# Hybrid Mamba, mixture-of-experts and gated-attention block: the softplus of later groups summed by accumulating transfers, the experts' weight rows issued from ACT, and new priorities for the planner

## The chip, the cores and the metric

One core of one Trainium2 chip. The metric is the device time of one execution in microseconds. Engines are named as in the profile: PE is TensorE, DVE is VectorE, ACT is ScalarE, POOL is GpSimd, SP is SyncE, which only issues transfers. Each engine runs its own list of instructions strictly in order; a transfer that is issued by an engine stands in that engine's list, and the engine waits there until what the transfer needs is ready.

## The reference, cut to what matters

The input is x with 8 sequences of 256 tokens and 128 features, all in float32. Four blocks follow each other, each added to its own input after a layer norm:

1. a selective state-space block (Mamba): RMS norm, a projection to 2 x 256 channels, a causal convolution of 4 taps, a SiLU, a projection to a time step and to B and C (16 states), and a recurrence over the 256 tokens;
2. a mixture of 8 experts with inner width 352, the best 2 per token;
3. a gated attention unit with squared-ReLU scores;
4. the same mixture of experts again, with the same weights.

The part that the change touches in the first block is the softplus of the time step:

```python
delta = jax.nn.softplus(ts @ dt_w + dt_b)
def step(state, inp):
    dA = jnp.exp(A[None, :, :] * d_t[:, :, None])
    new = dA * state + d_t[:, :, None] * B_t[:, None, :] * h_t[:, :, None]
    y = jnp.einsum('bin,bn->bi', new, C_t) + D * h_t
```

and in the mixture of experts the share `w_e` of expert e in each token:

```python
inter = up_o * jax.nn.silu(gate_o)
out = out + w_e[:, None] * (inter @ w_down[e])
```

## The kernel before, in words

**Groups and lanes.** The 8 sequences form 4 groups of 2 (512 tokens). For each group the work is cut into lanes, written as Python generators that yield one operation at a time: `prelude` (s: norm, projection, convolution, time step, softplus), `recurrence` (m), `gating` (g), `ending` (f), `tail` (t: projection back) and `rest` (r: first mixture p, attention a, second mixture r). Two lanes serve all groups: `feeder` loads the rows of B and C and lets ACT make the decays, `adder` issues accumulating transfers from POOL.

**The order of the work** is decided while the program is built. `Board` keeps, for each engine, when it would be free, and for each tile when it would be ready and when its last reader would be done, from costs that are written into the operations. `Board.pick` takes the lane whose next operation could start first; lanes on the same engine that could start no later than `PATIENCE` after it compete by rank (`RANKS`, one number per kind of lane and group; the lowest wins). An ACT operation that needs another activation table than the one that is loaded is held to start `SWITCH` = 1.3 later, but only if it has been ready for less than `LONG`; both `PATIENCE` and `LONG` are 0 before. Where PE would idle ahead of an operation, `Board.do` puts small matmuls of the identity into that operation's own output bank (`fill` in `pe`, line 324; one per 0.23 of planned idle time); they compute nothing that is kept. So the number of these fills in the program tells how long the planner expected PE to idle, and where.

**The recurrence.** For 2 of the 16 states and one half of the channels at a time, DVE multiplies B by delta*h (L743), scans (L748) and multiplies by C (L752), 1024 columns each; there are 16 such steps in each group. All but the first of the results in each half are summed into the first by transfers with accumulation (`adder`, L715, POOL queue, 512 KB each; five tiles hold such states). ACT makes the decays, exp(A*delta), ahead of the scans (L696).

**Softplus.** softplus(z) is put together as relu(z) + ln(1 + exp(-|z|)), plus a term for what 1 + e loses when it is rounded. ACT makes |z| (L595), relu(z) (L603), e (L613), w = 1 + e (L617) and ln w (L627). DVE makes the lost part in one operation (L621), subtracts it from both halves of relu(z) (L623), adds ln w to both halves (L631), and multiplies by h (L632). In groups 1 to 3 these take both halves (1024 columns) at once where they can; group 0 goes by halves.

**The mixture of experts.** Expert widths are laid end to end and cut into 22 tiles of 128. For each tile `gate` (a matmul, L486, and a SiLU on ACT, L958), `up` (L984, or L991 where a tile holds the border of two experts; its product with the SiLU is made on DVE, L998) and `down` (L1004) are issued, the gate 4 tiles ahead. The input of `up` is x already scaled by the expert's share: the shares are transposed, copied by ACT (L1019) and written to a small table in device memory (`wrow`, L1022), and row e of that table is loaded into all partitions (`fetched`, L967, 256 KB) and multiplied by x on DVE (L975). Both transfers are issued by POOL. Three tiles hold such rows, so the row of expert e+3 can be loaded only after the last `up` that reads expert e, the border matmul L991 (or L984). For the mixtures named in `SOON` the row of expert 0 is made by PE instead (L931, L938).

The activation sets are two: SiLU and tanh in one, exp and ln in the other; each change is an ACT_TABLE_LOAD (L57).

Of the kernel before, what the change touches and what calls it, by code (L numbers as in the profile page):

```python
# [31 lines left out]
class Board:  # L32
# [1 line left out]


    SWITCH = 1.3
    PATIENCE, LONG = 0, 0
    FILL = 0.23

    def given(self, op):  # L40
# [32 lines left out]
    def pick(self, lanes):  # L73

        at = []
        for l in lanes:
            t = self.start(l.op)

            if self.switches(l.op) and t - self.given(l.op) < self.LONG:
                t += self.SWITCH  # L80
            at.append((t, l))
        first, lane = min(at, key=lambda x: x[0])
        near = [
            l for t, l in at if l.op.engine == lane.op.engine and t <= first + self.PATIENCE
        ]
        return min(near, key=lambda l: l.rank)


class Lane:
    def __init__(self, rank, work, after):  # L90
        self.rank, self.work, self.after, self.op = rank, work, after, None


@with_exitstack
def kernel(
# [27 lines left out]
    nc = tc.nc  # L123
# [23 lines left out]
    BEHIND = 2  # L147

    RANKS = {
# [3 lines left out]
    }  # L153
    SOON = ("p0", "p1", "r0", "p3", "r3")
    SPLIT = ()
# [116 lines left out]
        nc.gpsimd.memset(t[:, :, 0 : K - 1], 0.0)  # L272
    one = const.tile([P, 1], FP, name="one")
    nc.vector.memset(one, 1.0)


    board = Board(nc.scalar.preload_act_table_set)
# [110 lines left out]
    def layernorm(x, name, key, rms=False, parts=None):  # L388
# [13 lines left out]
        def moments_and_guard():  # L402
# [8 lines left out]

        parts = parts or [x]
        yield dve(0.46 * NT + 0.2, [st, mv, rstd], parts, moments_and_guard)
        yield pool(1.8, [rstd], [], lambda: nc.gpsimd.tensor_tensor(
            rstd.ap, rstd.ap, half[:, 0:NT], ALU.pow
        ))
        xn = ring(norm, [P, NT, H], f"xn{key}", f"xn_{name}")
# [72 lines left out]
    def biased(x, bias):  # L490

        NT = x.ap.shape[1]
        yield pool(1.2, [x], [], lambda: nc.gpsimd.tensor_tensor(
            x.ap, x.ap, bias.unsqueeze(1).to_broadcast([P, NT, H]), ALU.add
        ))

# [20 lines left out]
    def prelude(g):  # L517
# [67 lines left out]

        dl = [ring(mam, [P, G], f"dl{c}", f"dl_{g}_{c}", bufs=2) for c in range(NI)]
        ex = ring(mam, [P, NI, G], "ex", f"ex_{g}")
        for c in range(NI):  # L590
            ps = bank([P, G], f"dt_{g}_{c}")
            yield pe(mm(G), [ps], [ww], product(
                ps.ap, [(dt_w_sb[:, c * P : (c + 1) * P], xpj[:R, :])]
            ))
            yield act(act_us(G), [ex], [ps], lambda: nc.scalar.activation(  # L595
                ex.ap[:, c, :], ps.ap, AF.Abs, bias=col("dt_b", c)
            ))
            if g == 0:
                yield dve(dve_us(G), [dl[c]], [ps], lambda: nc.vector.tensor_scalar(
                    dl[c].ap, ps.ap, col("dt_b", c), 0.0, ALU.add, ALU.max  # L600
                ))
            else:
                yield act(act_us(G), [dl[c]], [ps], lambda: nc.scalar.activation(  # L603
                    dl[c].ap, ps.ap, AF.Relu, bias=col("dt_b", c)
                ))
            shut(ps)

        parts = [(c, c + 1) for c in range(NI)] if g == 0 else [(0, NI)]
        exs = [Held(ex.ap[:, a:b, :], ex.ready) for a, b in parts]
        wws = [Held(ww.ap[:, a:b, :], ww.used) for a, b in parts]  # L610
        du = [ring(mam, [P, G], f"du{c}", f"du_{g}_{c}", bufs=2) for c in range(NI)]
# [16 lines left out]
        for (a, b), w in zip(parts, wws):  # L628
            for c in range(a, b):
# [2 lines left out]
                    nc.vector.tensor_mul(du[c].ap, dl[c].ap, h[c].ap)  # L632

                yield dve(2 * dve_us(G), [dl[c], du[c]], [w, h[c]], step)
        if g > 0:

            for c in range(NI):
                yield act(act_us(G), [h[c]], [], lambda: nc.scalar.mul(h[c].ap, h[c].ap, col("D", c)))
        ex.used = max(e.used for e in exs)
        ww.used = max(w.used for w in wws)  # L640
        led_up[g] = bc, h, xT, dl, du

    def gating(g):

# [156 lines left out]
    def tail(g):  # L801
        gates.pop(g)
        bc, h, _, delta, du = led_up.pop(g)
        G = SIZES[g] * T
# [24 lines left out]
    def forked(rank, works):  # L829

        kids = [Lane(rank + (i,), w, []) for i, w in enumerate(works)]
        for l in kids:
            forks[0] += 1
            l.name = f"fork{forks[0]}"
        lanes.extend(kids)
# [107 lines left out]
    def moe(g, which, key, shared, ends):  # L943
# [20 lines left out]
        def fetched(e):  # L964

            wb = ring(ffn, [P, G], f"wb{key}", f"wb_{nm}_{e}", bufs=WB)
            yield load(3.6, [wb], [wrow], lambda: nc.gpsimd.dma_start(  # L967
                wb.ap, wrow.ap[e : e + 1, :].partition_broadcast(P)
            ), "POOL", 0.6)
            wx[e] = wb  # L970

        def weighted(e):
# [36 lines left out]
        def tile_of(i):  # L1009
# [12 lines left out]
        yield load(2.2, [wrow], [weT], lambda: nc.gpsimd.dma_start(  # L1022
            wrow.ap.rearrange("e (t p) -> (e t) p", p=P), weT.ap
        ), "POOL", 0.7)


        for i in range(LEAD):
# [210 lines left out]
    for g in range(NG):  # L1238
# [5 lines left out]
        waiting[-1].name = f"g{g}"  # L1244
        waiting.append(Lane((RANKS["f"][g], g), ending(g), [f"m{g}"]))
        waiting[-1].name = f"f{g}"
        waiting.append(Lane((RANKS["t"][g], g), tail(g), [f"f{g}", f"g{g}"] + [f"t{g - 1}"] * (g > 0)))
        waiting[-1].name = f"t{g}"
        waiting.append(Lane((RANKS["r"][g], g), rest(g), [f"t{g}"] + [f"r{g - 2}"] * (g > 1)))
# [58 lines left out]
```

## Time and profile before

| | us |
|---|---|
| median of 3 runs (764.91 to 766.28) | 766.09 |
| the profiled execution | 766.44 |
| its span on the core | 764.7 |
| busy in the span: PE / DVE / ACT / POOL | 739.0 / 569.0 / 439.3 / 129.5 |
| ACT_TABLE_LOAD, 96 in all | 123 |
| transfers, mean | 116 GB/s |

The span is what the hardware profiler saw on the core; the execution's own time is 1.7 us longer. A busy PE isn't a PE that does useful work, since the fills count as busy too: 556 of its 1591 matmuls are fills. A float32 matmul of 512 columns leaves two records in the trace, and so does a fill.

### The profile page before, as it was taken

What the parts mean: (1) busy time and instruction counts of PE and PEld (TensorE: products, weight loads), DVE (VectorE), ACT (ScalarE), POOL (GpSimd) and SP (SyncE); (2) the same over time, 40 slices, a digit from 0 to 9 for tenths busy, and PEclk for the clock granted to TensorE, in tenths of its full rate; (3) what the DMA queues carried; (4) which work ended last, traced back from release to release, by engine and by line L of the source; (5) the groups of instructions that cost most, each with busy time, mean ns of one, the idle gap of its engine ahead of it and who ended that gap; (6) DMA issues with size and microseconds to landing.
All of it is one profiled execution on the core that took longest, in us unless ns stands there. A gap on an engine that the chain in (4) does not pass through costs nothing.

```text
span 764.7 us, 8437 instructions
## 1 busy us (share of the span) xinstructions
PE 739.0 (97%) x3077; PEld 402.2 (53%) x3077; DVE 569.0 (74%) x824; ACT 439.3 (57%) x576; POOL 129.5 (17%) x177
## 2 busy tenths in 40 slices
PE   4999999999989989999999999999999999999997
PEld 3877996664326654334654443343764433454343
DVE  2599999998999988899998997996636333535332
ACT  4578334698993787997776768742062321432221
POOL 2021110421212321111222221112101100200000
PEclk9999999999999999999999999999999999999999
DMA  8619795567865435476674557665000210101110
GB/s 257 207 60 219 178 219 143 141 143 175 218 147 132 87 101 134 110 180 136 145 186 111 132 129 181 164 153 109 1 28 29 69 28 14 28 14 44 27 42 14
DMA packets 34999, 88.63 MB, mean 116 GB/s; under 512 B 4339, under 2 KB 14414, under 8 KB 34958
## 3 DMA queue, kind: packets, MB, share of 16 engines
q0 software_dynamic: 14288, 46.54, 30.0%
q1 hardware_dynamic: 20624, 41.54, 16.5%
q8 instruction: 24, 0.39, 0.2%
q14 instruction: 17, 0.14, 0.1%
q10 hardware_dynamic: 46, 0.01, 0.0%
HBM read 55.71 MB, written 1.44 MB: 75 GB/s over the span
## 4 chain that ended last, share of the span: by engine, by line
PE 65%; DVE 21%; DMA 4%; issue 4%; ACT 4%; POOL 0%; DVEq 0%; ACTq 0%; POOLq 0%
PE dn_r L1004 10%; PE gp_r L486 9%; PE dn_p L1004 8%; DVE st L748 7%; PE up_r L984 7%; PE gp_p L486 6%; PE up_p L984 5%; DVE st L743 4%; DVE st L752 4%; PE up_r L991 3%; DMA wb_p<-wrow_p 3%; PE up_p L991 3%; PE av_a L1195 1%; PE xpj L324 1%; ACT L57 1%
## 5 line engine op out<-in xcount | busy, mean ns | idle before, releaser
L748 DVE TENSOR_TENSOR_SCAN st<-decay,st 128x1024 f32<-128x1024 f32 x64 | 147.3, 2302 | 2.9
L57 ACT ACT_TABLE_LOAD x95 | 121.9, 1283 | 1.7
L696 ACT ACTIVATE decay<-dl,zero,a_sb 128x510 f32<-128x510 f32 x128 | 96.8, 806 | 42.8 <-DVE st L748 42.1
L958 ACT ACTIVATE sg_r<-gp_r,zero 128x512 f32<-128x512 f32 x88 | 60.1, 687 | 104.7 <-PE gp_r L486 92.6
L998 DVE TENSOR_TENSOR it_r<-up_r,sg_r 128x512 f32<-128x512 f32 x88 | 60.4, 687 | 66.6 <-PE up_r L984 40.7
L958 ACT ACTIVATE sg_p<-gp_p,zero 128x512 f32<-128x512 f32 x88 | 59.2, 686 | 62.8 <-PE gp_p L486 45.3
L1004 PE MATMUL dn_p<-it_p,wd_sb 128*128 128x512 f32 x176 | 91.0, 604 | 3.6 <-DVE it_p L998 3.5
L715 POOL DMA_DIRECT2D st<-st x58 | 51.0, 885 | 241.9 <-DVE st L752 199.2
L1004 PE MATMUL dn_r<-it_r,wd_sb 128*128 128x512 f32 x176 | 90.4, 601 | 0.0
L486 PE MATMUL gp_r<-xT_r,wg_sb 128*128 128x512 f32 x176 | 89.4, 594 | 0.0
L998 DVE TENSOR_TENSOR it_p<-up_p,sg_p 128x512 f32<-128x512 f32 x88 | 59.9, 685 | 39.1 <-PE up_p L984 26.0
L486 PE MATMUL gp_p<-xT_p,wg_sb 128*128 128x512 f32 x176 | 88.8, 593 | 0.0
L743 DVE TENSOR_TENSOR st<-bt,du 128x1024 f32<-128x1024 f32 x64 | 78.8, 1231 | 0.0
L752 DVE TENSOR_TENSOR st<-st,ct 128x1024 f32<-128x1024 f32 x64 | 78.1, 1220 | 0.8
L984 PE MATMUL up_p<-wb_p,wu_sb 128*128 128x512 f32 x128 | 65.4, 595 | 0.5 <-DVE wb_p L975 0.5
L984 PE MATMUL up_r<-wb_r,wu_sb 128*128 128x512 f32 x128 | 65.4, 596 | 0.0
L1004 PEld LDWEIGHTS dn_p<-it_p,wd_sb 128*128 128x128 f32 x176 | 31.6, 189 | 51.0 <-issue 35.9
L486 PEld LDWEIGHTS gp_p<-xT_p,wg_sb 128*128 128x128 f32 x176 | 33.0, 190 | 40.6 <-issue 35.9
L486 PEld LDWEIGHTS gp_r<-xT_r,wg_sb 128*128 128x128 f32 x176 | 32.9, 190 | 40.7 <-issue 35.4
L1004 PEld LDWEIGHTS dn_r<-it_r,wd_sb 128*128 128x128 f32 x176 | 31.7, 190 | 41.9 <-issue 35.5
L324 PEld LDWEIGHTS y<-ident 128*128 128x128 f32 x464 | 52.1, 192 | 1.2 <-PE dt L486 0.8
L324 PE MATMUL y<-ident 128*128 128x128 f32 x464 | 52.4, 275 | 0.0
(225 smaller groups left out, 885.1 us busy)
## 6 DMA issues: line engine op xcount, KB each, us to landing
st<-st POOLq DMA_DIRECT2D x54, 512.0 KB, 6.4
bt<-bc SPq DMA_DIRECT2D x32, 512.0 KB, 5.7
ct<-bc SPq DMA_DIRECT2D x32, 512.0 KB, 4.9
wb_r<-wrow_r POOLq DMA_DIRECT2D x30, 256.0 KB, 3.9
wb_p<-wrow_p POOLq DMA_DIRECT2D x29, 256.0 KB, 4.8
st<-h POOLq DMA_DIRECT2D x6, 256.0 KB, 3.8
wg_sb<-in_L_ffn_w_gate_dram SPq DMA_DIRECT2D x2, 704.0 KB, 4.3
wu_sb<-in_L_ffn_w_up_dram SPq DMA_DIRECT2D x2, 704.0 KB
```

The costliest lines, as they stand in the source:

```text
L57: self.load_tables(op.table)
L324: nc.tensor.matmul(ps[:, 0:n], lhsT=ident[:, 0:m], rhs=ident[:, 0:n], start=True, stop=True)
L486: nc.tensor.matmul(ps, lhsT=lhsT, rhs=rhs, start=(i == 0), stop=(i == len(terms) - 1))
L696: nc.scalar.activation(shaped[:, n, :, 1:], delta[c].ap.rearrange("p (b t) -> p b t", b=GB)[:, :, 1:], AF.Exp, bias=zero, scale=a_sb[:, c, ...
L715: yield load(us, [acc], [st], lambda: nc.gpsimd.dma_start(into, of, accum_op=ALU.add), "POOL", 0.9)
L743: yield dve(1.22, [st], [bt, du[c]], lambda: nc.vector.tensor_mul(st.ap, bt.ap, du[c].ap.unsqueeze(1).to_broadcast([P, NC, G])))
L748: yield dve(2.29, [st], [das[c]], lambda: nc.vector.tensor_tensor_scan(flat, das[c].ap.rearrange("p n t -> p (n t)"), flat, 0.0, ALU.mult, ...
L752: yield dve(1.22, [st], [ct], lambda: nc.vector.tensor_mul(st.ap, st.ap, ct.ap))
L958: yield act(act_us(G), [sg], [gp], lambda: nc.scalar.activation(sg.ap, gp.ap, AF.Silu, bias=zero), SILU)
L984: nc.tensor.matmul(ps.ap, lhsT=wu_sb[:, i * P : (i + 1) * P], rhs=wa.ap[:, cols_of], start=True, stop=True,)
L998: yield dve(dve_us(width), [it], [ps, sg], lambda: nc.vector.tensor_mul(it.ap, ps.ap, sg.ap[:, cols_of]))
L1004: yield pe(mm(dn.ap.shape[1]), [dn], [it], lambda: nc.tensor.matmul(dn.ap, lhsT=wd_sb[:, i, :], rhs=it.ap[:, cols_of], start=(i == 0), sto ...
```

## The change

1. **Softplus of groups 1 to 3.** relu(z) of both halves lies in one tile (`dl`). ACT makes w = -1 - e with a new constant `minus_one`, DVE makes (w + 1) + e, which is the lost part with its sign turned, and ACT makes ln(-w). The lost part and the logarithm are then added to `dl` by two accumulating transfers of 512 KB each, issued by POOL through `adder`, one after the other; DVE only multiplies by h once both have landed. The four DVE operations L623 and L631 go in each of these groups. Group 0 stays as it was.
2. **Rows of the experts.** The write of the table and the loads of its rows are issued by ACT instead of POOL; the planner's time for issuing goes from 0.6 and 0.7 to 0.1.
3. **The planner.** `PATIENCE` is 0.21 and `LONG` is 2.6; each lane has its own patience, which is a new number per group (`"w"`) for the lanes of `ending` and for the forked lanes; all ranks are new; the planned cost of the power on POOL is 1.45 (was 1.8) and of the bias on POOL 1.6 (was 1.2). So nearly all instructions of later stages stand in another order.

```diff
-    PATIENCE, LONG = 0, 0
+    PATIENCE, LONG = 0.21, 2.6
...
-            l for t, l in at if l.op.engine == lane.op.engine and t <= first + self.PATIENCE
+            l for t, l in at if l.op.engine == lane.op.engine and t <= first + l.patience
...
-        "s": [4, 4, 1, 2.5], "m": [1.5, 3.5, 3, 3.5],
-        "g": [2, 0, 1.5, 2], "t": [1, 0, 0, 0.5],
-        "r": [2.5, 0.5, 3.5, 2.5], "f": [1, 0, 4, 0.5], "feeder": 5, "adder": 1.5,
+        "s": [3, 2, 3.5, 2.5], "m": [3.5, 4, 4, 2.5],
+        "g": [4, 2.5, 2.5, 0.5], "t": [1, 3, 0, 0.5],
+        "r": [2.5, 1, 2.5, 2], "f": [1, 0, 4, 0], "w": [0, 0, 1.5, 0], "feeder": 5, "adder": 0,
...
-        yield pool(1.8, [rstd], [], lambda: nc.gpsimd.tensor_tensor(
+        yield pool(1.45, [rstd], [], lambda: nc.gpsimd.tensor_tensor(
...
-        yield pool(1.2, [x], [], lambda: nc.gpsimd.tensor_tensor(
+        yield pool(1.6, [x], [], lambda: nc.gpsimd.tensor_tensor(
...
-        dl = [ring(mam, [P, G], f"dl{c}", f"dl_{g}_{c}", bufs=2) for c in range(NI)]
+        both = ring(mam, [P, NI, G], "dl", f"dl_{g}", bufs=2)
+        dl = [Held(both.ap[:, c, :], both.used) for c in range(NI)]
...
+        if g > 0:
+            both.ready = max(d.ready for d in dl)
+            both.used = max(d.used for d in dl)
+            yield act(act_us(NI * G), [ex], [], lambda: nc.scalar.activation(
+                ex.ap, ex.ap, AF.Exp, bias=zero, scale=-1.0
+            ), EXP)
+            yield act(act_us(NI * G), [ww], [ex], lambda: nc.scalar.activation(
+                ww.ap, ex.ap, AF.Identity, bias=minus_one, scale=-1.0
+            ))
+            yield dve(dve_us(NI * G), [ex], [ww], lambda: nc.vector.scalar_tensor_tensor(
+                ex.ap, ww.ap, 1.0, ex.ap, ALU.add, ALU.add
+            ))
+            sums.append((f"s{g}", 6.3, both, ex, both.ap, ex.ap))
+            yield act(act_us(NI * G), [ww], [], lambda: nc.scalar.activation(
+                ww.ap, ww.ap, AF.Ln, bias=zero, scale=-1.0
+            ), EXP)
+            sums.append((f"s{g}", 6.3, both, ww, both.ap, ww.ap))
+            while landed.get(f"s{g}", 0) < 2:
+                yield None
+            du = [ring(mam, [P, G], f"du{c}", f"du_{g}_{c}", bufs=2) for c in range(NI)]
+            for c in range(NI):
+                dl[c].ready = both.ready
+                yield dve(dve_us(G), [du[c]], [dl[c], h[c]], lambda: nc.vector.tensor_mul(
+                    du[c].ap, dl[c].ap, h[c].ap
+                ))
+                yield act(act_us(G), [h[c]], [], lambda: nc.scalar.mul(h[c].ap, h[c].ap, col("D", c)))
+            led_up[g] = bc, h, xT, dl, du
+            deltas[g] = both
+            return
...
-            yield load(3.6, [wb], [wrow], lambda: nc.gpsimd.dma_start(
+            yield load(3.6, [wb], [wrow], lambda: nc.scalar.dma_start(
                 wb.ap, wrow.ap[e : e + 1, :].partition_broadcast(P)
-            ), "POOL", 0.6)
+            ), "ACT", 0.1)
...
-        yield load(2.2, [wrow], [weT], lambda: nc.gpsimd.dma_start(
+        yield load(2.2, [wrow], [weT], lambda: nc.scalar.dma_start(
             wrow.ap.rearrange("e (t p) -> (e t) p", p=P), weT.ap
-        ), "POOL", 0.7)
+        ), "ACT", 0.1)
```

The line numbers of the profile are those of the kernel before; in the changed kernel these lines stand 3 to 36 further down.

More of the change, by code (lines that the diff above doesn't have):

```diff
@@ L91, in __init__ @@
         self.rank, self.work, self.after, self.op = rank, work, after, None
+        self.patience = Board.PATIENCE
 @with_exitstack
@@ L274 @@
     nc.vector.memset(one, 1.0)
+    minus_one = const.tile([P, 1], FP, name="minus_one")
+    nc.vector.memset(minus_one, -1.0)
     board = Board(nc.scalar.preload_act_table_set)
@@ L606, in prelude @@
             shut(ps)
-        parts = [(c, c + 1) for c in range(NI)] if g == 0 else [(0, NI)]
+        if g > 0:
[27 more added lines that the diff above has]
+            return
+        parts = [(c, c + 1) for c in range(NI)]
         exs = [Held(ex.ap[:, a:b, :], ex.ready) for a, b in parts]
@@ L634, in prelude @@
                 yield dve(2 * dve_us(G), [dl[c], du[c]], [w, h[c]], step)
-        if g > 0:
-            for c in range(NI):
-                yield act(act_us(G), [h[c]], [], lambda: nc.scalar.mul(h[c].ap, h[c].ap, col("D", c)))
         ex.used = max(e.used for e in exs)
@@ L641, in prelude @@
         led_up[g] = bc, h, xT, dl, du
+        deltas[g] = both
+    deltas = {}
     def gating(g):
@@ L803, in tail @@
         bc, h, _, delta, du = led_up.pop(g)
+        deltas[g].used = max(d.used for d in delta)
         G = SIZES[g] * T
@@ L832, in forked @@
         for l in kids:
+            l.patience = RANKS["w"][rank[1]]
             forks[0] += 1
@@ L1246 @@
         waiting[-1].name = f"f{g}"
+        waiting[-1].patience = RANKS["w"][g]
         waiting.append(Lane((RANKS["t"][g], g), tail(g), [f"f{g}", f"g{g}"] + [f"t{g - 1}"] * (g > 0)))
```

## The prediction

> **What bounds the kernel now.** I read the page's 40 slices first, then the chain, then PE's fills stage by stage, then the single waits.
>
> ```profile
> PE   4999999999989989999999999999999999999997
> DVE  2599999998999988899998997996636333535332
> ACT  4578334698993787997776768742062321432221
> PE 65%; DVE 21%; DMA 4%; issue 4%; ACT 4%; POOL 0%; DVEq 0%; ACTq 0%; POOLq 0%
> ```
>
> PE looks full everywhere, yet the chain starts on DVE. The next answers split it: busy time by stage, of PE's fills alone (line 324) and of all engines.
>
> ```profile
> 0.00:128.00 128.00, 85.67 (x738) 85.03 (x738) 1.00 0.69 185
> 128.00:281.00 153.00, 31.11 (x256) 30.52 (x256) 1.00 0.62 147
> 281.00:543.00 262.00, 6.59 (x50) 6.20 (x50) 0.99 0.58 137
> 543.00:765.00 222.00, 8.49 (x68) 8.30 (x68) 1.00 0.10 29
> ...
> 128.00:281.00 153.00, 144.47 (x640) 84.12 (x640) 142.74 (x208) 121.37 (x151) 37.37 (x40) 1.00 0.62 147
> 281.00:543.00 262.00, 261.18 (x862) 116.45 (x863) 230.68 (x302) 181.71 (x223) 51.09 (x67) 0.99 0.58 137
> ```
>
> The columns of a stage are its length, PE, PE's weight loads, and in the last two lines DVE, ACT and POOL; (x) counts records, two per fill. Up to 128 us PE is mostly fills: group 0's recurrence runs on DVE alone. From 128 to 281 DVE is busy 143 of 153 us, and it is the bound. From 281 on PE is full, and the fills (118 records, 59 fills) are all that is left to win there; idle time outside them is under 1 us up to the last matmul. So the end is: when DVE lets PE start at 281, plus PE's fixed work, plus the fills after it.
>
> The waits that the change aims at, on POOL, PE and DVE in the first mixture:
>
> ```profile
> 162.53 0.56 POOL L1022 DMA_DIRECT2D wrow_p<-weT_p  x1
> 168.63 0.87 POOL L715 DMA_DIRECT2D st<-st  x1 [5.54 <-DVE st L752]
> 169.30 1.34 POOL L967 DMA_DIRECT2D wb_p<-wrow_p  x2
> 167.53 7.53 PE L324 MATMUL up_p<-ident 128*128 128x128 f32 x66
> 176.84 0.69 DVE L975 TENSOR_TENSOR wb_p<-wb_p,xT_p 128x512 f32<-128x512 f32 x1 [2.41 <-DMA wb_p<-wrow_p]
> ```
>
> The rows' load stands in POOL's list behind a state sum that waits 5.54 us for DVE; PE fills for 7.5 us and DVE waits 2.41.
>
> **The change part by part.**
>
> ```profile
> L57 ACT ACT_TABLE_LOAD x95 | 121.9, 1283 | 1.7
> L623 DVE TENSOR_TENSOR dl<-dl,ex 128x512 f32<-128x512 f32 x8 | 5.3, 689 | 0.2
> L631 DVE TENSOR_TENSOR dl<-dl,ww 128x512 f32<-128x512 f32 x8 | 5.4, 680 | 0.0
> st<-st POOLq DMA_DIRECT2D x54, 512.0 KB, 6.4
> bc<-ww SPq DMA_DIRECT2D x4, 64.0 KB, 4.8
> 1.91 0.28 ACTq L206 DMA_DIRECT2D vecs<-in_L_attn_a_conv_b_dram  x1
> L681 SPq DMA_DIRECT2D bt<-bc x32: 319/320/1638, 28.5 to 491.1; - x32
> ```
>
> *Softplus.* Four DVE operations go in each of three groups. They start 0.60 to 0.70 us apart, so 2.4 us per group. Two transfers per group come in: a 0.885 us issue on POOL and 6.4 us to land each, the second after the first, 14.6 us where DVE took 2.4. In the changed order DVE's multiply by h of group 1 stands three recurrence steps after the lost part's operation (4.79 us each, from the state sums' issues, which come 4.79 apart): 14.4 us of cover. So group 1 gains its 2.4, called 2.3, as group 0 is alone on DVE. If both landed at the 9.3 us that is the longest sum here, it would lose some 6 (2 x 10.2 - 14.4). Behind the pair on POOL two state sums wait; two spare tiles cover one more step. ACT does as many operations as before.
>
> *Middle stage.* Added up row by row from the instruction order, with the trace's spacing of starts (a recurrence step 4.7, a 512-column operation 0.60), DVE has 143.7 us of work from group 0's last gate product (127.4) to the first up product of group 1's first mixture (280.25). That took 152.9, so DVE waited 9.2. In the changed kernel the same span holds 147.8: two more scans, group 3's convolution and the dropped operations less. That is +4.1, and as much less later.
>
> Of the 9.2 us of waits, 5.9 are for expert rows (2.41 here, 0.92 at 206 and 2.59 at 280). On ACT the load no longer stands behind a state sum, but the table's write could be slower: the write from SP's list took 4.8 us for 64 KB, POOL's took 2.1 for 16 KB, so +2.7 at worst, with four SiLUs (2.7 us) between the write and the load in the new order. Gain between 0 and 5.9; I take half, 3.0, since one part of each wait is the landing itself. Nothing comes of row waits after 281, where PE stays full.
>
> *ACT's new transfers.* 59 rows and 8 tables at 0.28 (ACT's small loads) to 0.32 (SP's row broadcasts, the same form): 18.8 to 21.4 us more in ACT's list. Loads of tables fall from 96 to 80 in the order: 16 x 1.283 = 20.5 us less. Even, and ACT has 32 us of slack in the middle stage and 80 in the next. A row's wait for the border matmul now holds ACT: behind it stand SiLUs of the next gates, which PE runs after that border anyway, so 0; but 6 of the 35 rows that are issued while the recurrence runs have a table load and a decay right behind. At the mean wait of a SiLU for its gate (92.6 us in 54 waits, 1.7) these are 10 us of ACT, part of it under the three decay tiles that are made ahead. Bounds 0 and 10; I take 2.
>
> The Trainium skill (ScalarE: Activation LUTs, What ACT_TABLE_LOAD costs) counts a drain with each load, 2.66 us per switch. By it the 16 loads would be 42.6 us. The trace doesn't show the drain: a load starts at 163.42 and the next SiLU at 164.72. The skill (DMA: Bandwidth & Descriptors, Issuing engines are not separate DMA queues) also speaks against the move: another issuing engine saves only issue time. By that the 3.0 above would be 0; the 5.54 us ahead of the row's load is a wait in POOL's list, which the rule doesn't count.
>
> *POOL and traffic.* POOL loses 38.7 us of issues and gains 5.3; it is busy 17%, so nothing. The six transfers add 3.1 of 88.6 MB; B and C rows are loaded when DVE frees a tile and are waited for by no DVE row above 1 us: nothing.
>
> *The order.* Fills are instructions and can be counted: 556 before, 534 after. Up to group 0's projection back 403 become 387 (the softplus again); in the middle 94 become 124; from there on 59 become 23. One takes 0.225 us (255 records in 28.64 us). In the last part, where planned and real idle time agree, 36 x 0.225 = 8.1 us go: the 15 fills ahead of group 1's attention products become 5, and the 17 ahead of the last group's first transposes go. The middle's 30 more fills stand where PE waits for DVE anyway, so I count that stage by DVE.
>
> *Sum.* -2.3 + 4.1 - 3.0 - 8.1 + 2.0 = -7.3 us. From the profiled execution's 766.44 (span 764.7 and 1.7 around it) that is 759.1; it stands 0.35 above the median, so 758.8.
>
> **The rivals.**
> 1. *ACT's held list becomes the bound (slower).* Each of the 35 rows before the recurrence's end holds ACT, the decays come late, and DVE's scans wait. For it: of the 42.1 us that ACT waited for a free decay tile (a scan not yet done), only 3.4 lie from 131 to 300 and 4.2 from 300 to 560, so decays are made barely ahead there. Against: the slack above. Without holds the sum is -9.3, so it decides from 0.27 us per row on; at 0.4 each, 14 us, 771; at 0.5, 774.
> 2. *The middle's fills are real.* 30 x 0.225 = 6.8 us there instead of 4.1 - 3.0: 764.5. For it: the planner's fills of the last part came true before. Against: DVE's work doesn't call for them.
> 3. *The transfer pair lands late* in group 1, at 9.3 us each: 6 more, 764.8. For it: two other sums are in flight at that time; against: sums there land in about 6.2.
>
> **How the numbers follow.** Forecast 0.47, rival 1 0.26, rival 2 0.16, rival 3 0.11. Range 750 to 773: below, the full 5.9 for row waits and no holds give 754, and 4 more if the wait time that isn't for rows goes too; above, rival 1 at 0.5 less a bit. The forecast's own range is 753 to 764. A measurement here tells 0.2% (1.5 us) from no change. Rivals 2 and 3 lie at that border: faster 0.62, same 0.09, slower 0.29.
>
> **What would show it.** Right: fills after about 280 near 46 records instead of 118; table loads 79 in the group of line 57; group 0's gate product near 125; no fill of 7.5 us ahead of the first mixture's third up tile. ACT's wait of transfers for border matmuls should be small, and DVE's scans should wait for decays as little as now (2.9 us before L748). Wrong: scans idle 10 us or more for decays; PE idle after 281 without fills; or the multiply by h of group 1 idle for a transfer.

## The result, and the profile after

The changed kernel takes 761.36 us (median of 5 runs, 760.57 to 765.34), the kernel before 766.09 (5 runs, 764.85 to 766.92): a ratio of 0.9945, 95% interval 0.9928 to 0.9963. It is 4.7 us faster; the forecast was 7.3. The runs of the changed kernel lie further apart than those of before, and its profiled execution is the slowest of the five: 765.34, span 763.6, only 1.1 below the profiled span of before. So that profile shows what can go wrong as well as what was won.

The fills of PE (line 327 now) by the same stages as before, then all engines in the two middle stages (the columns are those explained in the prediction):

```profile
0.00:128.00 128.00, 80.70 (x700) 80.36 (x700) 0.97 0.74 191
128.00:281.00 153.00, 37.37 (x310) 36.87 (x310) 1.00 0.66 156
281.00:543.00 262.00, 4.32 (x32) 4.12 (x32) 1.00 0.60 141
543.00:765.00 222.00, 3.55 (x26) 3.37 (x26) 1.00 0.10 29
...
128.00:281.00 153.00, 148.63 (x697) 90.00 (x696) 144.82 (x205) 107.88 (x140) 32.86 (x31) 1.00 0.66 156
281.00:543.00 262.00, 258.30 (x846) 114.32 (x845) 230.33 (x307) 176.41 (x221) 35.35 (x39) 1.00 0.60 141
```

After 281 us 58 fill records are left of 118, and their time falls from 15.08 to 7.87 us. In the first stage the granted clock of PE is 0.97, where it was 1.00. Three marks cut an execution into the stages of the prediction: group 0's last gate product on DVE (L830, before L796), group 1's first up product (L1034, before L998), and the last addition to x (L481, before L478). Read off the timeline of DVE:

| profiled execution | group 0's last gate product | middle stage | last part | time |
|---|---|---|---|---|
| before | 127.42 | 152.83 | 480.20 | 766.44 |
| changed | 132.30 (+4.88) | 154.98 (+2.15) | 472.27 (-7.93) | 765.34 |
| predicted difference | -2.3 | +1.1 | -6.1 | -7.3 |

The last part did as predicted and a little better; the first stage went the other way. Its place is seen in the timeline of POOL and of DVE in the changed kernel, each line with its start, its duration and, in brackets, how long the engine idled before it and for what:

```profile
75.49 1.22 DVE L621 SCALAR_TENSOR_TENSOR ex<-ww,ex 128x1024 f32<-128x1024 f32 x1
77.01 0.86 POOL L749 DMA_DIRECT2D dl<-ex  x1 [0.28 <-DVE ex L621]
87.03 0.86 POOL L749 DMA_DIRECT2D dl<-ww  x1 [9.16 <-ACT decay L730]
87.58 2.11 POOL L749 DMA_DIRECT2D st<-st  x2
94.27 1.29 DVE L634 TENSOR_TENSOR du<-dl,h 128x512 f32<-128x512 f32 x2 [3.26 <-DMA dl<-ww]
97.38 1.23 DVE L777 TENSOR_TENSOR st<-bt,du 128x1024 f32<-128x1024 f32 x1 [1.82 <-DMA st<-st]
97.89 0.87 POOL L749 DMA_DIRECT2D st<-st  x1 [8.21 <-DMA st<-st]
```

The first transfer of group 1's softplus is issued at 77.01; the second, which adds to the same tile, is issued ten microseconds later, with two state sums right behind it. (The page puts POOL's wait down to a decay; POOL's second transfer needs the first one landed and the logarithm written.) DVE waits 3.26 us for the second transfer and then 1.82 us for a free state tile, because the two sums behind it are late too. That is 5.08 us of waits for the 2.4 us of DVE work that was dropped: rival 3, with the additional wait for a tile.

PE then pays as well. Its fills ahead of group 0's sum over the states were laid for the planned time; here they run out, PE idles, and the next four matmuls (eight records) take 5.40 us where they took 3.70 before (first line, the kernel before), so that DVE's gate product waits 0.70:

```profile
117.38 3.70 PE L486 MATMUL y<-st,ident 128*128 128x512 f32 x8
...
121.47 5.40 PE L489 MATMUL y<-st,ident 128*128 128x512 f32 x8 [3.81 <-DVE st L786]
...
126.91 0.69 DVE L830 TENSOR_TENSOR du<-y,g 128x512 f32<-128x512 f32 x1 [0.70 <-PE y L489]
```

The rows of the experts now hardly keep DVE waiting, and table loads and scans are as predicted. First the kernel before, then the changed kernel (busy time, mean ns, and behind the second bar the idle time ahead of these operations with what ended it):

```profile
L975 DVE TENSOR_TENSOR wb_r<-wb_r,xT_r 128x512 f32<-128x512 f32 x30 | 20.4, 684 | 7.1 <-DMA wb_r<-wrow_r 7.1
L975 DVE TENSOR_TENSOR wb_p<-wb_p,xT_p 128x512 f32<-128x512 f32 x29 | 19.8, 684 | 15.5 <-DMA wb_p<-wrow_p 15.5
```

```profile
L57 ACT ACT_TABLE_LOAD x79 | 101.4, 1283 | 5.2 <-issue 2.5 <-PE up_p L1027 1.1 <-ACT weT_r L1055 0.4
L782 DVE TENSOR_TENSOR_SCAN st<-decay,st 128x1024 f32<-128x1024 f32 x64 | 147.2, 2300 | 3.0
L1011 DVE TENSOR_TENSOR wb_r<-wb_r,xT_r 128x512 f32<-128x512 f32 x30 | 20.5, 684 | 2.8 <-DMA wb_r<-wrow_r 2.7
L1011 DVE TENSOR_TENSOR wb_p<-wb_p,xT_p 128x512 f32<-128x512 f32 x29 | 19.8, 683 | 1.4 <-DMA wb_p<-wrow_p 1.4
...
dl<-ex POOLq DMA_DIRECT2D x3, 512.0 KB, 8.4
dl<-ww POOLq DMA_DIRECT2D x3, 512.0 KB, 5.5
```

In groups 2 and 3 the multiply by h (L634) waits 0.28 and 0 us for its transfers: the cover is long enough there.

### The profile page after: what moved, and what is told of

It is laid out like the page before. It is cut to its first block, busy times and chain, and to the rows that moved or that the text cites. A ratio compares the mean times of both kernels' runs of the same rounds, so it can differ in the third digit from the quotient of the medians.

```text
span 763.6 us, 8337 instructions
## 1 busy us (share of the span) xinstructions
PE 733.6 (96%) x3033; PEld 397.9 (52%) x3033; DVE 562.8 (74%) x813; ACT 419.3 (55%) x560; POOL 96.5 (13%) x116
## 4 chain that ended last, share of the span: by engine, by line
PE 62%; DVE 4%; DMA 2%; ACT 1%; POOL 1%; issue 1%; ACTq 0%; POOLq 0%; DVEq 0%
PE dn_r L1040 10%; PE gp_r L489 10%; PE dn_p L1040 7%; PE up_r L1020 7%; PE gp_p L489 7%; PE up_p L1020 5%; PE up_r L1027 3%; PE up_p L1027 2%; PE av_a L1231 2%; PE v_a L1165 1%; PE u_a L489 1%; DMA st<-st 1%; PE sc_a L1210 1%; DVE st L782 1%; DMA wb_r<-wrow_r 1%; PE pb_a L508 1%
## 5 line engine op out<-in xcount | busy, mean ns | idle before, releaser
L1034 DVE TENSOR_TENSOR it_r<-up_r,sg_r 128x512 f32<-128x512 f32 x88 | 60.5, 687 | 68.4 <-PE up_r L1020 43.5
L1034 DVE TENSOR_TENSOR it_p<-up_p,sg_p 128x512 f32<-128x512 f32 x88 | 60.2, 685 | 47.0 <-PE up_p L1020 26.1
L327 PEld LDWEIGHTS y<-ident 128*128 128x128 f32 x486 | 54.7, 192 | 1.7 <-issue 1.0
L327 PE MATMUL y<-ident 128*128 128x128 f32 x486 | 55.0, 275 | 0.0
```

The costliest lines, as they stand in the source:

```text
L327: nc.tensor.matmul(ps[:, 0:n], lhsT=ident[:, 0:m], rhs=ident[:, 0:n], start=True, stop=True)
L1034: yield dve(dve_us(width), [it], [ps, sg], lambda: nc.vector.tensor_mul(it.ap, ps.ap, sg.ap[:, cols_of]))
```

## The experiments

My theory after the result: the gain comes from the last part's fills and from the rows on ACT, and a part of it is lost in group 1's chained pair of transfers. Its rivals: the loss in group 1 is an accident of the slowest execution; the queue that issues the rows hardly matters; the new order by itself is the gain. The times are medians, each with the ratio to the kernel before on the same chip.

| run | us | ratio (95%) | fills in the program |
|---|---|---|---|
| changed, once more | 762.88 | 0.9955 (0.9938 to 0.9972) | 534 |
| group 1's softplus on DVE | 761.07 | 0.9931 (0.9918 to 0.9943) | 546 |
| one transfer in group 1 | 760.49 | 0.9925 (0.9913 to 0.9938) | 539 |
| all softplus on DVE | 783.56 | 1.0247 (1.0223 to 1.0271) | 634 |
| before, rows on ACT, order kept | 762.88 | 0.9958 (0.9944 to 0.9973) | 556 |
| before, rows on ACT, planned so | 766.26 | 0.9990 (0.9982 to 0.9999) | 582 |
| changed, rows on POOL, order kept | 768.72 | 1.0023 (1.0007 to 1.0039) | 534 |
| changed, rows on POOL, planned so | 793.36 | 1.0348 (1.0319 to 1.0377) | 610 |
| before with the new numbers | 776.23 | 1.0132 (1.0115 to 1.0148) | 595 |
| before with the softplus transfers | 776.16 | 1.0122 (1.0095 to 1.0150) | 553 |
| one transfer, power planned longer | 760.74 | 0.9933 (0.9921 to 0.9945) | 539 |
| one transfer, 20 fills fewer | 760.49 | 0.9927 (0.9915 to 0.9939) | 519 |

And the stages of their profiled executions, by the same marks as above:

| profiled execution | group 0's last gate product | middle | last part |
|---|---|---|---|
| before | 127.42 | 152.83 | 480.20 |
| changed, once more | 130.41 | 153.35 | 472.30 |
| group 1's softplus on DVE | 129.61 | 153.37 | 472.43 |
| one transfer in group 1 | 127.70 | 153.35 | 473.38 |
| all softplus on DVE | 128.88 | 162.98 | 483.73 |
| before, rows on ACT, order kept | 127.85 | 149.30 | 481.16 |
| before, rows on ACT, planned so | 127.58 | 142.22 | 489.88 |
| changed, rows on POOL, order kept | 132.71 | 155.98 | 474.77 |
| changed, rows on POOL, planned so | 130.18 | 167.69 | 486.19 |
| before with the new numbers | 128.53 | 161.62 | 478.35 |
| before with the softplus transfers | 132.14 | 156.06 | 485.80 |
| one transfer, power planned longer | 128.17 | 153.50 | 472.04 |
| one transfer, 20 fills fewer | 129.24 | 153.37 | 472.07 |

### Is the loss in group 1 an accident?

The changed kernel without an edit:

> The changed kernel once more. In its profiled execution DVE waited 3.26 us for the transfer of the logarithm and 1.82 us for a free state tile in group 1's softplus, and group 0's last gate product stood at 132.3 us (before 127.4). Theory 1, these waits belong to the program: they come again, 4 to 6 us together, the gate product again near 132, time 761. Theory 2, they are an accident of one execution, and the landing of two transfers varies from run to run: under 2 us of waits, gate product at 125 to 128, time 759 to 761.

762.88 us, the six runs from 760.15 to 765.12. The waits came again, though smaller, 0.80 and 2.80 us:

```profile
92.19 1.29 DVE L634 TENSOR_TENSOR du<-dl,h 128x512 f32<-128x512 f32 x2 [0.80 <-DMA dl<-ww]
96.28 1.23 DVE L777 TENSOR_TENSOR st<-bt,du 128x1024 f32<-128x1024 f32 x1 [2.80 <-DMA st<-st]
...
120.37 3.70 PE L489 MATMUL y<-st,ident 128*128 128x512 f32 x8 [2.33 <-DVE st L786]
```

The gate product at 130.41 lies between the two theories, the sum of the waits (3.6) just under the first one's 4 to 6. The pair is late in both profiles, by amounts that differ. The stages add up to what was gained here: +3.0, +0.5, -7.9 is -4.4 us, and this execution took 761.87, 4.6 less than the profiled one of before.

Next, group 1's softplus on DVE as before, and all else in the order of the changed kernel:

```diff
-        if g > 0:
+        if g > 1:
             both.ready = max(d.ready for d in dl)
...
-        parts = [(c, c + 1) for c in range(NI)]
+        parts = [(c, c + 1) for c in range(NI)] if g == 0 else [(0, NI)]
...
+        if g > 0:
+            for c in range(NI):
+                yield act(act_us(G), [h[c]], [], lambda: nc.scalar.mul(h[c].ap, h[c].ap, col("D", c)))
         ex.used = max(e.used for e in exs)
```

> The changed kernel, but the softplus of group 1 is put together by DVE as before (groups 2 and 3 by transfers). On each engine the order is otherwise that of the changed kernel. DVE gets back four operations of 0.60 us. Theory 1, the transfers of group 1 cost in every execution what the profile shows (5.1 us of waits against 2.4 us saved): 2.7 us less than the changed kernel, 758 to 759, group 0's last gate product near 129. Theory 2, the waits are an accident of the profiled execution: 2.3 us more, 763 to 764.

761.07, the five runs within 1.2 us of each other (760.33 to 761.52). On the same chip that is 1.8 us less than the changed kernel, although DVE does 2.4 us more work. The gate product stands at 129.61 (129 expected), the other two stages are the same to 0.1. The 2.7 of theory 1, and its 758 to 759, were not reached; they were worked out from the slowest execution. Theory 2 wanted 763 to 764 and is out. But the ratio's interval still overlaps that of the repeat, so the difference in time is likely and not certain; what the profiles show is that the two waits are gone. Whether the spread of the changed kernel (5.2 us over its 11 runs) comes from the pair is open: the kernel with all softplus on DVE, which has no pair, spreads over 6.7 us in five runs.

Then only half of it: the lost part stays a transfer, the logarithm goes back to DVE.

```diff
-            sums.append((f"s{g}", 6.3, both, ww, both.ap, ww.ap))
-            while landed.get(f"s{g}", 0) < 2:
+            if g > 1:
+                sums.append((f"s{g}", 6.3, both, ww, both.ap, ww.ap))
+            while landed.get(f"s{g}", 0) < 1 + (g > 1):
                 yield None
...
+                def step():
+                    if g == 1:
+                        nc.vector.tensor_add(dl[c].ap, dl[c].ap, ww.ap[:, c, :])
+                    nc.vector.tensor_mul(du[c].ap, dl[c].ap, h[c].ap)
```

> The changed kernel, but in group 1 only the lost part is added by a transfer; the logarithm is added by DVE (two operations of 0.60 us) just ahead of the multiply by h, where the changed kernel has it. Else the order is the same. Theory 1, it is the second transfer of the chain that comes late, and the state sums queued behind it: with one transfer the waits of 3.6 to 5.1 us go to under 0.5, group 0's last gate product near 127.5 to 128.5, 1 us ahead of the kernel with group 1 on DVE: 759.5 to 760.5. Theory 2, any such transfer at that place slows the state sums: waits of 2 us or more stay, 761 to 763.

760.49, and the gate product at 127.70. One wait is left:

```profile
85.07 0.69 DVE L638 TENSOR_TENSOR dl<-dl,ww 128x512 f32<-128x512 f32 x1 [0.29 <-DMA dl<-ex]
85.80 0.69 DVE L639 TENSOR_TENSOR du<-dl,h 128x512 f32<-128x512 f32 x1
```

With one transfer no state sum is late; the two small edits of this version below show the same (waits of 0.54 and 0.42 us for the transfer, none for a tile). So it is the chain of two, with the sums that are listed behind it, that costs, and not any transfer at that place. This version has the lowest median of all, with the two small edits of it below; its interval overlaps that of the kernel with group 1 on DVE, so between these nothing is claimed. Both have lower medians than the changed kernel, but the intervals of all three touch or overlap.

### Which queue issues the rows, with the order held still

The rows were moved between ACT's and POOL's lists while the planner was told nothing of it, so that PE's, DVE's and SP's instructions keep their order exactly. In the changed kernel back to POOL:

```diff
-            yield load(3.6, [wb], [wrow], lambda: nc.scalar.dma_start(
+            yield load(3.6, [wb], [wrow], lambda: nc.gpsimd.dma_start(
                 wb.ap, wrow.ap[e : e + 1, :].partition_broadcast(P)
             ), "ACT", 0.1)
...
-        yield load(2.2, [wrow], [weT], lambda: nc.scalar.dma_start(
+        yield load(2.2, [wrow], [weT], lambda: nc.gpsimd.dma_start(
```

> The changed kernel with the table's write and the rows issued by POOL, but planned as if ACT issued them at 0.1: PE's, DVE's and SP's instructions stay in exactly the order of the changed kernel (534 fills), and the 67 transfers move from ACT's list to POOL's at the same place in the program. Theory 1, POOL's list delays the rows: DVE's waits for rows rise from 4.1 us (changed kernel) to 15 or more, and the time goes to 768 to 790. Theory 2, the issuing queue hardly matters and the planner's order is the gain: 761 to 764. Theory 3, the holds of ACT cost the 2.0 us that the prediction gave them and POOL's list costs less: 759 to 761.

768.72: all of the gain is gone, and more; it is 5.8 us above the repeat of the changed kernel. Of the 7.7 us between the two profiled executions (769.56, the slowest of its six, and 761.87), 2.3 lie in group 1's stage, before any row is loaded (a start that is 0.19 later, 0.25 more of waits for the pair, and 1.78 in which DVE waits for PE after an idle time of 4.28 us); the middle is 2.6 and the last part 2.5 us longer, so that 5.1 us can be put down to the queue. DVE waited 10.9 us for rows (6.5 and 4.4; 2.4 in the repeat), not the 15 that theory 1 named.

And the other way, the kernel before with its rows issued by ACT, at the old planned costs:

```diff
-            yield load(3.6, [wb], [wrow], lambda: nc.gpsimd.dma_start(
+            yield load(3.6, [wb], [wrow], lambda: nc.scalar.dma_start(
                 wb.ap, wrow.ap[e : e + 1, :].partition_broadcast(P)
             ), "POOL", 0.6)
...
-        yield load(2.2, [wrow], [weT], lambda: nc.gpsimd.dma_start(
+        yield load(2.2, [wrow], [weT], lambda: nc.scalar.dma_start(
```

> The kernel before with the table's write and the rows issued by ACT, and planned as before: the order on PE, DVE and SP is exactly that of before (556 fills). Theory 1, the rows no longer stand behind state sums: of the 22.6 us that DVE waits for rows, 15 or more go, of which the prediction counts 3.0 (0 to 5.9) in the middle stage: 760 to 764. Theory 2, in this order ACT has no room and its holds for border matmuls delay decays and SiLUs: 768 to 775. Theory 3, the issuing queue doesn't matter: 765 to 767.

762.88: two lines give 3.5 us of the 4.7 that the whole change gives. The middle stage, where the prediction counted 3.0, is 3.5 shorter, and DVE's waits for rows in it fall from 5.9 to 2.8. But theory 1 also said that 15 of all 22.6 us of these waits would go, and that was wrong; by groups of instructions they are 31.3 in this run:

```profile
L975 DVE TENSOR_TENSOR wb_r<-wb_r,xT_r 128x512 f32<-128x512 f32 x30 | 20.5, 683 | 16.5 <-DMA wb_r<-wrow_r 16.5
L975 DVE TENSOR_TENSOR wb_p<-wb_p,xT_p 128x512 f32<-128x512 f32 x29 | 19.8, 682 | 14.8 <-DMA wb_p<-wrow_p 14.8
```

Most of them lie after 281 us, where PE is full: the last part takes 481.16 instead of 480.20. A wait that grew by 12 us there cost at most 1. Theory 2, ACT held up, shows nowhere: the scans wait 2.9 us for decays in both kernels.

### The parts, each replanned

With all softplus on DVE again, in the changed kernel (the condition above as `if g > 9`):

> The changed kernel with all softplus parts put together by DVE as before, replanned: 634 fills (362, 209 and 63 by stages; changed kernel 350, 155, 29). Theory 1, the relief of DVE in groups 2 and 3 (2.4 us each) and the order planned around it carry the gain: 34 more fills at the end are 7.7 us, the middle 4.8 us longer, group 1's stage 2 shorter: 769 to 774. Theory 2, the transfers bring nothing, as their waits eat what DVE saves: 758 to 763.

783.56, outside both theories. The group 1 stage is better, the middle has DVE busy 154.0 us instead of 146.6 and is 9.6 longer, and the last part 11.4 longer, of which the 34 fills that are added are 7.7. The prediction's additive view (2.4 us of DVE for a group) gives 4.8 of this; the rest goes with the order that the planner finds without the transfers, and was not taken apart.

The rows on POOL, and planned so:

> The changed kernel with the table's write and the experts' rows issued by POOL again, at the planned costs of before. The planner lays 610 fills instead of 534: 350, 171 and 89 by the same stages (changed kernel 350, 155, 29). Theory 1, POOL's list delays the rows and the planner's fills after group 1 are real idle time: 60 x 0.225 = 13.5 more, 772 to 778, DVE's waits for rows back to near 22 us. Theory 2, only the rows' waits of the middle stage return: 3 to 6 more, 764 to 767. Theory 3, which engine issues matters only by its issue time, which is hidden on both: 760 to 763.

793.36, 15 above the highest theory. Compared with the repeat of the changed kernel, the last part is 13.9 us longer (60 fills were 13.5) and the middle 14.3, where 16 fills more were planned (3.6) and DVE waits 9.7 us for rows.

The planner's numbers alone, in the kernel before:

```diff
-    PATIENCE, LONG = 0, 0
+    PATIENCE, LONG = 0.21, 2.6
...
-        "s": [4, 4, 1, 2.5], "m": [1.5, 3.5, 3, 3.5],
+        "s": [3, 2, 3.5, 2.5], "m": [3.5, 4, 4, 2.5],
...
-        yield pool(1.8, [rstd], [], lambda: nc.gpsimd.tensor_tensor(
+        yield pool(1.45, [rstd], [], lambda: nc.gpsimd.tensor_tensor(
```

> The kernel before with the planner's new numbers alone (patience, held tables, ranks, the two planned costs on POOL). Fills are 595 instead of 556: 362 up to group 0's projection back, 166 until group 1's first up product, 67 after it (before 362, 123, 71). Theory 1, the new order by itself brings the gain of the last part, 8 us: 757 to 760. Theory 2, the gain needs the rows on ACT, since after group 1 the planned fills hardly fall (71 to 67): 762 to 768, and the 43 more in the middle cost up to 9.7 (at 0.225): 775.

776.23: 9.8 us slower than before. Theory 1 is out. Of the combinations that were run, the new numbers are fast only with the rows on ACT and the transfers together: without the transfers the time was 783.56, without the rows on ACT 793.36.

The softplus transfers alone, in the kernel before:

> The kernel before with the softplus of groups 1 to 3 put together by transfers, and nothing else; replanned, 553 fills (356, 120, 77; before 362, 123, 71). Theory 1, stage by stage: group 1's pair costs what two profiles of the changed kernel show, 3.6 to 5.1 us of waits against 2.4 saved (+1 to +3), the middle and the rest change by no more than the fills (6 more at the end, 1.4): 767 to 770. Theory 2, DVE's relief in groups 2 and 3 shows as it should have in the middle stage: -2.4 or more there, 762 to 766.

776.16, 9 us slower, worse than either theory. The profiled execution is the slowest of the six (780.22, 13.8 above the profiled one of before). In it the pair of group 1 is late as in the changed kernel, and DVE's gate product waits 1.74 us for PE (+4.7 up to there); the middle is 3.2 and the last part 5.6 longer. The order and the granted clock, 0.96 from 128 to 281 us, go with these; what each costs was not separated:

```profile
93.06 1.29 DVE L633 TENSOR_TENSOR du<-dl,h 128x512 f32<-128x512 f32 x2 [2.87 <-DMA dl<-ww]
96.17 1.23 DVE L776 TENSOR_TENSOR st<-bt,du 128x1024 f32<-128x1024 f32 x1 [1.81 <-DMA st<-st]
...
128.00:281.00 153.00, 146.22 (x614) 84.71 (x613) 140.78 (x201) 116.73 (x146) 37.57 (x40) 0.96 0.63 146
```

The rows on ACT in the kernel before, this time planned so:

> The kernel before with the rows on ACT, this time planned so (0.1 on ACT), ranks as before: 582 fills (362, 155, 65; before 362, 123, 71). Where only the issuing queue was changed and the order kept, the time was 762.9. Theory 1, planned fills tell the time, here as in the other replanned kernels: 26 more than before at 0.225 are 5.9 us, less the 3.5 that the queue brings: 766 to 772. Theory 2, what the planner knows of the queue helps it: below 762.9.

766.26: no difference to before that counts. DVE's waits for rows are down to 0.3 and 0.9 us, the middle is 10.6 shorter and the last part 9.7 longer: work has moved across the mark, and the replanned order gives back all that the queue had brought (762.88 with the old order). It is at the lower end of theory 1, which counts fills.

So fills in the program rank these kernels only roughly: those with 519 to 546 are the fast ones as long as ACT issues the rows, 582 and 556 are equal, and 553 is 9 us slower than 556.

### Two small terms

The planned time of group 1's power on POOL, 1.9 instead of 1.45, in the version with one transfer:

```diff
-        yield pool(1.45, [rstd], [], lambda: nc.gpsimd.tensor_tensor(
+        yield pool(1.9 if name == "m1" else 1.45, [rstd], [], lambda: nc.gpsimd.tensor_tensor(
```

> The kernel with one transfer in group 1's softplus (760.49), and the power on POOL of group 1's norm planned at 1.9 instead of 1.45 (its measured time is 1.86). The order changes at that place alone: DVE's small operation that waits for this power goes behind the first scan again, as in the kernel before. Theory 1, its wait of 0.91 us stands on the path: group 0's last gate product 0.9 earlier, near 126.8, and 759.4 to 759.9. Theory 2, it moves into a later wait and nothing is won: 760.3 to 760.8.

760.74: no difference. The wait itself is gone; first the version without this edit, then the one with it:

```profile
40.23 1.86 POOL L417 TENSOR_TENSOR rstd_m<-rstd_m,half 128x4 f32<-128x4 f32 x1 [15.98 <-DVE rstd_m L409]
42.13 0.16 DVE L433 SCALAR_TENSOR_TENSOR shift_m<-mv_m,rstd_m 128x4 f32<-128x4 f32 x1 [0.91 <-POOL rstd_m L417]
42.21 2.29 DVE L787 TENSOR_TENSOR_SCAN st<-decay,st 128x1024 f32<-128x1024 f32 x1
```

```profile
42.43 2.29 DVE L787 TENSOR_TENSOR_SCAN st<-decay,st 128x1024 f32<-128x1024 f32 x1
44.63 0.14 DVE L433 SCALAR_TENSOR_TENSOR shift_m<-mv_m,rstd_m 128x4 f32<-128x4 f32 x1
```

But this execution reached its first operation on the time step (`dl<-dt`) at 29.87 instead of 28.77 us; counted from there the gate product comes 0.63 earlier. In the profiled executions this start lies between 28.27 and 29.87, more than the term is worth, and the medians can't show it.

Twenty fills fewer ahead of group 0's sum over the states, in the version with one transfer:

```diff
-            for _ in range(int((idle - 0.3) / self.FILL)):
+            n = int((idle - 0.3) / self.FILL)
+            for _ in range(n - 20 if n > 150 else n):
```

> The kernel with one transfer in group 1's softplus, with 20 fills fewer ahead of group 0's sum over the states (187 instead of 207), all else in the same order. PE then idles some 4.5 us (20 x 0.225) there, where it did not before. Theory 1, the idle time itself lowers the granted clock (after an idle of 2.33 us the eight matmuls of that sum took 3.70 us, after 2.79 and more 5.40 to 6.47): 5.40 or more here too, the granted clock of 120 to 130 us under 0.9, DVE's gate product waits 0.7 or more for PE, and the time is 0.5 to 2 above 760.49. Theory 2, the clock fell for another reason (the transfers under way at that time): 3.60 to 3.70, no wait, 760 to 761.

760.49, the same median, but the profile answers the question. Here PE idles 3.69 us, and the same four matmuls take 5.40 with a granted clock of 0.83 from 118 to 128 us; with the fills they take 3.60 at 1.00. First with fewer fills, then with all:

```profile
118.41 5.40 PE L493 MATMUL y<-st,ident 128*128 128x512 f32 x8 [3.69 <-DVE st L795]
123.84 0.69 DVE L839 TENSOR_TENSOR du<-y,g 128x512 f32<-128x512 f32 x1 [0.70 <-PE y L493]
...
118.00:128.00 10.00, 9.59 (x20) 4.34 (x21) 9.06 (x7) 2.16 (x3) 0.00 (x0) 0.83 0.43 133
```

```profile
118.42 3.60 PE L489 MATMUL y<-st,ident 128*128 128x512 f32 x8
...
118.00:128.00 10.00, 10.00 (x37) 5.46 (x36) 9.73 (x8) 2.95 (x4) 0.00 (x0) 1.00 0.43 122
```

The idle time lowers the clock, and DVE waits 0.70 for it, as theory 1 said. The gate product stands at 129.24 instead of 127.70; 0.59 of this is a later start (29.36 instead of 28.77). What the wait costs in the end is too little for the medians: the 0.5 to 2 us of that theory did not come.

## Why the prediction was right, and where it was wrong

The direction, the likeliest case and the range were right, and the time is 2.6 us above the forecast. By its own steps:

- **Fills of the last part (-8.1).** Right in the main. 30 fills fewer (60 records) came, where 36 were counted, and 7.2 us less of them. The last part is 7.9 shorter in both profiles: 2.7 us of other work of PE moved ahead of the mark, and PE idles 2.0 us more. To count fills in the program that was to be run, and only in the stage where planned and real idle time agree, held; in kernels that were replanned for the experiments the same count was off by 10 us and more.
- **Middle stage, DVE's work (+4.1).** Right: DVE is busy 146.77 instead of 142.57 us between the marks, 4.2 more.
- **Middle stage, row waits (-3.0 of 0 to 5.9).** Right, and tested by itself: -3.2 in waits and -3.5 in the stage with the order kept. In the changed kernel 5.9 became 1.1 (0.6 in the repeat), but the other idle time of DVE grew by 2.8 (1.8). The stage came out 2.15 and 0.5 longer in its two profiles (predicted 1.1). From ACT the write of the first mixture's table landed in 2.9 us (median of 4; from POOL 2.1), so 0.8 of the 2.7 that were feared.
- **ACT held at border matmuls (+2.0).** Wrong, too high: nothing of it is seen. ACT's SiLUs do wait for row transfers (18.2 us in five places), but PE is full behind them, and the scans wait 3.0 us for decays, as before (2.9). Rival 1, at 0.26, was given too much.
- **Softplus, group 1 (-2.3).** Wrong, and this is the step that failed. The transfers were to cost nothing, since a cover of 14.4 us was set against 14.6 for two landings of 6.4; and behind the pair, two spare tiles were to cover one more step. From the issue of the first transfer to DVE's multiply it took 17.3 us in the profiled execution and 14.8 in the repeat, 14.0 of them covered: waits of 3.26 and 0.80. The tiles did not cover the step behind: 1.82 and 2.80 us of waits for a tile. That second wait is the steadier one, 1.81 to 2.80 in all five profiles with the pair, while the multiply waited in four of them (0.80 to 3.26) and not in the fifth, with the rows planned on POOL. The prediction's own sign of being wrong, the multiply by h of group 1 idle for a transfer, was seen, and the gate product stood at 132.30 and 130.41 and not near 125. Rival 3 with its 0.11 named the place, and the first of the two waits only.
- **What was not in the sum.** The planned cost of the power, 1.45 against a real 1.86, puts DVE's `shift_m` ahead of a scan, 0.91 us in all kernels that plan it so; and PE's clock after an idle time, 0.70 in the profiled execution and nothing in the repeat. In the repeat the stage up to group 0's last gate product is 0.58 (later start) + 0.91 - 2.4 + 3.6 of waits, 2.7 of the 3.0 that were measured.

That the net came within 2.6 us is in part luck. By the stages of the repeat, the first went 5.3 us against the forecast (+3.0 instead of -2.3); the last part, where the 2.0 of ACT did not come, gave back 1.8, and the middle 0.6. What the sum could not say is which of the three parts matters: rows alone, order kept, give -3.5; the softplus and the numbers, each alone and replanned, +9 and +9.8. The parts don't add.

Open: why the pair's transfers land later in group 1 than the sums' median of 6.4 us was not tried by itself, nor whether the two state sums would be in time if POOL's list held them ahead of the second transfer. Nor was it measured what the transfers of groups 2 and 3 bring with the order kept: only the replanned kernel without them was run.

## What to carry to other kernels

Where a planner writes the order, keep the order still to measure one part: move one instruction to another queue without telling the planner, and compare that with the replanned kernel; here 762.88 and 766.26 for the same edit. Two transfers that add to the same tile are a chain, and everything behind them in the issuing list is late with them: ask for a cover that holds the longest landing in the profile, twice, and count the transfers behind. A wait of an engine matters only in the stage where that engine sets the end: 12 us more of DVE's row waits cost at most 1, and 3 us less of them elsewhere gave 3.5.

## What the runs showed of the hardware

PE's granted clock falls after short idle times, and not always after the same ones. Ahead of group 1's convolution PE idles 2.25 us in nine of the profiled executions. In six of them the four matmuls (eight records) behind it took 5.40 us, in three 3.70. First the changed kernel, then that with group 1's softplus on DVE:

```profile
59.34 5.40 PE L489 MATMUL conv<-padded,taps_sb 128*128 128x512 f32 x8 [2.25 <-ACT padded L538]
```

```profile
60.19 3.70 PE L489 MATMUL conv<-padded,taps_sb 128*128 128x512 f32 x8 [2.25 <-ACT padded L538]
```

Ahead of group 0's sum over the states, 2.33 us left it at 3.70; 2.79, 3.69 and 3.81 gave 5.40, and 3.82 and 4.28 gave 6.44 and 6.47. In the kernel with all softplus on DVE, after 3.37 us ahead of an up matmul, the first matmul still took 1.12 us; the clock fell 1.3 us after it had begun, and the next ones of 512 columns took 1.61 and 1.75 where 1.02 is usual.

The records of the granted clock in the traces show what decides it. Every fall is to half and lasts 3.41 us or two or three times that (60.19 to 63.60 in the changed kernel), and from its first rise on the clock changes only at whole multiples of 3.41 us. So the time can be cut into stretches of 3.41 us, counted from that rise, which comes 14.7 to 17.7 us after the start. Of the 2.25 us of idle time, the part in one stretch was 1.97 to 2.25 us in the six executions with a fall and 1.64 to 1.88 in the three without; the 2.33 us that did nothing were cut in halves by a border. Over the 14 profiled executions up to 750 us, each stretch at full clock in which PE idled 1.96 us or more (18 of them) was followed by half clock, and none with 1.88 or less was, but for two falls in the kernel before with the softplus transfers. At half clock less was enough: 1.02 us of idle time or more in such a stretch kept the clock down for another (five times; 1.27 and 1.21 us in the cases with 6.44 and 6.47), and 0.30 or less did not. Idle time here is that between PE's recorded matmuls; fills count as matmuls. The Trainium skill (TensorE: Matmul & The Clock Gate, HAM oscillation — how this bites in real kernels) gives gaps over about 3.4 us as those to avoid; here 2.25 was enough in six executions.

Issued from ACT, a row's load takes 0.326 us of the list, from POOL 0.56 to 0.63 in the mean. The Trainium skill (DMA: Bandwidth & Descriptors, Issuing engines are not separate DMA queues) says that another issuing engine saves only such time; moving 67 transfers with the order kept was worth 3.5 us in one kernel (medians) and 5.1 in the other (middle and last part of the profiles), where POOL's list held state sums that wait for DVE between the rows.
